# A scan layer's recurrence with part of its work on GpSimd, C turned ahead of it, and the last spectral pass with DRAM tiles of its own

## The chip, the cores and the metric

The kernel runs on one core of one Trainium2 chip. The metric is the device time of one execution in microseconds (us). TensorE (PE) multiplies matrices into PSUM, VectorE (DVE), ScalarE (ACT) and GpSimd (POOL) do the elementwise work, and SyncE (SP) issues most DMA transfers; ACT issues some.

## The reference

One image of 48 x 48 positions with 768 channels, f32, passes through four layers: an attention block, a spectral layer (a 2-D FFT, a two-layer network by blocks of 96 channels on every mode, the inverse FFT), a scan layer, and a second spectral layer with the same formula. What the change touches is the scan layer and the two spectral ones. The scan, shortened:

```python
B, C = silu(x @ W_B + ...), silu(x @ W_C + ...)      # 64 channels n x 4 ranks r
X = silu(x @ W_X + b_X);  alpha = sigmoid(x @ W_dec + b_dec)
theta = x @ W_th + b_th;  gamma = sigmoid(x @ W_lam + b_lam)
Hst, prev = 0, None
for i in range(12):
    inj = _rope(B, theta * (i + 1)) * X              # channel pairs turned by an angle
    Hst = diffuse(Hst)                               # 3x3 convolution, one filter per channel
    if prev is None: Hst = alpha * Hst + inj
    else: Hst = alpha * Hst + (1 - gamma) * alpha * prev + gamma * inj
    prev = inj
return silu((_rope(C, theta * 12) * Hst) @ W_out + b_out)
```

## The kernel before

The four layers follow one another on the core, and almost everything is f32. TensorE does the projections, the convolution (as products with banded matrices) and the FFTs (as products with matrices of sines). Instructions on each engine run in the order in which a scheduler puts them; `tc.keep_in_program_order` pins an instruction to its place in the program.

**Rows.** In the scan the 48 image rows lie in two halves on the partitions (48 columns at partition 0, 48 at partition 64, so 112 partitions are used, K), and 24 row pairs lie along the free axis (NPR).

**Projections** (`scan_phase`, line 1180 on). Eight chunks q of three row pairs each. TensorE writes a chunk's 357 columns for C, decay, angle, X and gamma and 256 for B into PSUM (line 1273); VectorE adds the biases into `za` and `g` (line 1274). Then the chunk's chain runs on VectorE and ScalarE: the angle is reduced and its sine and cosine are taken (`sincos`), g is multiplied by X (line 1299), B is turned by theta with `turn` (line 1475) into `i0` through two helper tiles m0 and m1, and H's first value is written (line 1310). Then the angle times 12 gets its own sine and cosine (from line 1311), and C with these is stored in DRAM as `c_d` (lines 1313, 1314). Last come the two states s0 and s1 (lines 1338 to 1344), with which the recurrence builds the injection without any more sines: the next state is `2 cos(theta) * s - previous s`.

**Recurrence** (`step` and `after`, lines 1364 to 1399). Eleven iterations `it` by eight groups `gr` of eight channels are 88 steps. A step is 64 recorded matmuls of H with the bands (line 1373), VectorE's product with alpha in PSUM (line 1375) and its sum with the state, written to H (line 1377). GpSimd forms `t = s * c1` (line 1381), ScalarE copies t over the PSUM bank just read (line 1382), and `after`, one step later, subtracts the older state (line 1393). There are four PSUM tiles, `pss[gr % 4]`. In the last iteration t and the subtraction fall away, and H is multiplied by the turned C (line 1399). The bands of groups 1 to 7 are loaded by SP just before the first step (line 1356), and ScalarE repeats alpha over the ranks into `alr`.

**C's turn by 12 theta** runs on GpSimd during the recurrence: `c_turned` loads a chunk from `c_d`, does `turn`'s six operations and stores `cr_d`; the loop over the steps advances it by one operation where `i % 4` is not zero. The last iteration reads `cr_d`.

**After the scan** comes the transposition of H (line 1443) and the output projection (line 1460).

**Spectral layers** (`spectrum_mix`). The FFT along the rows has put a spectrum into `yu` in DRAM. Items (group, kc, block) pass four stages with lags of 0, 1, 3 and 4 steps: FFT along the columns (line 1685), the two layers of the network (1699 to 1721), and the inverse (f_u, line 1736), evicted to `us` and handed to `put`. `keep_warm` (line 139) issues matmuls that nobody reads; three of them stand ahead of the first step, two at steps 1 and 2, and twelve behind the last step in `afno_second`. In `afno_second`, the last layer, each of four groups is two blocks of 96 channels; `put` stores a result to `yu` (line 1931), `reload` brings it back turned (line 1936) and `back` does the inverse FFT along the rows (line 1960) and stores the output (line 1950). For the final group the order of transfers is pinned; the second last kc's reload is issued together with the last one's:

```python
elif group == final and kc != NKC - 2:
    for k in (kc,) if kc < NKC - 1 else (kc - 1, kc):
        for b in range(2):
            reload(nc.scalar if k == NKC - 1 and b else nc.sync, b, chunk(k), 0, G // 2)
```

Of the kernel before, what the change touches and what calls it, by code (L numbers as in the profile page):

```python
# [21 lines left out]
G = 48  # L22
# [1157 lines left out]
def scan_phase(tc, ident, w, wts, rows_back, xh, x_close, c_d, cr_d, out_open):  # L1180
# [21 lines left out]
    NCR = NN * RR  # L1202
    NA = NCR + NN + NM + RR + 1
    V, GP = nc.vector, nc.gpsimd
    with tc.tile_pool(name="sc_s", bufs=1, side="left") as sp:
# [3 lines left out]
        def out_weights():  # L1209
            wp = out_open("so_w")  # L1210
            wo = wp.tile([P, 2, C], F32, tag="wo", name="wo")
            nc.sync.dma_start(wo, wo_d)
            return wo, load_bcast(nc, wp, bo_d, C, "bo", parts=K)

        with (
# [15 lines left out]
            with (  # L1231
                tc.tile_pool(name="sc_pw", bufs=1, side="left") as wp,
                tc.tile_pool(name="sc_pt", bufs=1, side="left") as tp,
            ):
                bias = load_bcast(nc, wp, b0_d, NA + NCR, "bias", pin=tc.keep_in_program_order)
                bias1 = load_bcast(nc, tp, b1_d, NA + NCR, "u", pin=tc.keep_in_program_order)
                V.tensor_tensor(bias, bias, bias1, ALU.add)
                cb = load_bcast(nc, wp, cb_d, NN, "cb", pin=tc.keep_in_program_order)
                halfpi = wp.tile([P, 1], F32, tag="halfpi", name="halfpi")
                V.memset(halfpi, math.pi / 2.0)  # L1240

                def temp(shape, tag, q, bufs=1):
                    return tp.tile([P, *shape], F32, tag=tag, name=f"{tag}_{q}", bufs=bufs)[:K]

                def sincos(th, q, nm):
                    r, a = reduce_angle(nc, tp, th, NM * R4, f"{nm}_{q}", K)
                    cs = temp([2, NM, R4], nm, q)
                    nc.scalar.activation(cs[:, 0].rearrange("p m t -> p (m t)"), a, AF.Sin, bias=halfpi[:K], scale=-1.0)
                    nc.scalar.activation(cs[:, 1].rearrange("p m t -> p (m t)"), r, AF.Sin)
                    return cs  # L1250

                def over_r(v, n):
                    return v.unsqueeze(2).to_broadcast([K, n, RR, R4])


                turn_of = itertools.cycle(range(2))
                banks = lambda tag: pss[3][:, next(turn_of), :]
                xs = [rows_back(0, banks)]
                for q in range(NQ):
                    prs = slice(q * R4, (q + 1) * R4)  # L1260
                    za = temp([NA, R4], "za", q, 2)
                    g = temp([NCR, R4], "g", q, 2)
                    for t in range(R4):
                        pr = q * R4 + t
                        if pr % 4 == 2 and pr + 4 < NPR:
                            xs.append(rows_back(pr // 4 + 1, banks))
                        x_of = lambda cc: (xs[pr // 4], cc, pr % 4 * P) if cc < NC // 2 else (xh, cc - NC // 2, pr * P)
                        ps = pss[pr % 3]
                        parts = ((za, 0, NA), (g, NA, NCR))
                        for i, (z, c0, n) in enumerate(parts):  # L1270
                            for cc in reversed(range(NC)):
                                v, c, tok = x_of(cc)
                                nc.tensor.matmul(ps[:K, i, :n], lhsT=v[:, c, tok : tok + K], rhs=w[:, cc, c0 : c0 + n], start=cc == NC - 1, stop=cc == 0)  # L1273
                        biased = [lambda z=z, c0=c0, n=n, i=i, t=t, ps=ps: V.tensor_tensor(z[:, :, t], ps[:K, i, :n], bias[:K, c0 : c0 + n], ALU.add) for i, (z, c0, n) in enumerate(parts)]
                        biased.pop(0)()
                        if t < R4 - 1:
                            biased.pop(0)()
                    last = q == NQ - 1
                    pin = tc.keep_in_program_order if last else lambda ins: ins

                    def silu():
                        pin(biased.pop(0)())
                        for t in (x, g, c):
                            pin(nc.scalar.activation(t, t, AF.Silu))

                    g3 = g.rearrange("p (n r) t -> p n r t", r=RR)
                    c, x = za[:, :NCR, :], za[:, NA - 1 - RR : NA - 1, :]
                    thz = za[:, NCR + NN : NCR + NN + NM, :]
                    alq = al[:K, :, prs]
                    ga = temp([1, R4], "ga", q)  # L1290
                    th = temp([NM * R4], "th", q)
                    if last:
                        silu()
                    V.tensor_copy(th, thz.rearrange("p m t -> p (m t)"))
                    cs = sincos(th, q, "t1")
                    if not last:
                        silu()

                    V.tensor_tensor(g.rearrange("p (n r) t -> p n (r t)", r=RR), g.rearrange("p (n r) t -> p n (r t)", r=RR), x.rearrange("p r t -> p (r t)").unsqueeze(1).to_broadcast([K, NN, RR * R4]), ALU.mult)
                    pin(nc.scalar.activation(alq, za[:, NCR : NCR + NN, :], AF.Sigmoid))  # L1300
                    pin(nc.scalar.activation(ga, za[:, NA - 1 : NA, :], AF.Sigmoid))
                    i0 = temp([NCR, R4], "i0", q)
                    i03 = i0.rearrange("p (n r) t -> p n r t", r=RR)
                    m = [temp([NM, RR, R4], f"m{j}", q) for j in range(2)]
                    for op in turn(V, i0, g, over_r(cs[:, 0], NM), over_r(cs[:, 1], NM), m):
                        op()

                    ac = temp([NN, R4], "ac", q)
                    V.tensor_tensor(ac, alq, cb[:K].unsqueeze(2).to_broadcast([K, NN, R4]), ALU.mult)
                    V.tensor_tensor(H[:K, :, :, 1 + q * R4 : 1 + (q + 1) * R4], i03, over_r(ac, NN), ALU.add)  # L1310
                    pin(V.tensor_scalar(th, th, float(ITERS), None, ALU.mult))  # L1311
                    cs12 = sincos(th, q, "t12")
                    nc.sync.dma_start(c_d[:K, q, :NCR], c)
                    nc.sync.dma_start(c_d[:K, q, NCR:].rearrange("p (s m) t -> p s m t", s=2), cs12)
                    c1q = c1[:K, :, prs]
                    pin(V.tensor_scalar(c1q, cs[:, 0], 2.0, None, ALU.mult))

                    def by_gamma(out, in_):
                        for t in range(R4):
                            nc.scalar.mul(out[:, :, t], in_[:, :, t], ga[:, 0, t : t + 1])  # L1320


                    om = temp([1, R4], "om", q)
                    pin(V.tensor_scalar(om, ga, -1.0, 1.0, ALU.mult, ALU.add))
                    be = temp([NN, R4], "be", q)
                    V.tensor_tensor(be, alq, om.to_broadcast([K, NN, R4]), ALU.mult)
                    bc = temp([NN, R4], "bc", q)
                    gc = temp([NM * R4], "th", f"{q}_g").rearrange("p (m t) -> p m t", t=R4)
                    V.tensor_tensor(gc, c1q, ga.to_broadcast([K, NM, R4]), ALU.mult)
                    for j in range(2):  # L1330
                        ms = slice(j * NM, (j + 1) * NM)
                        V.tensor_tensor(bc[:, ms], be[:, ms], gc, ALU.add)
                    flat = lambda v: v.rearrange("p n r t -> p (n r) t")

                    u = temp([NCR, R4], "u", q)
                    by_gamma(u, i0)
                    t0 = s0[:K, :, :, prs]
                    V.tensor_tensor(t0, g3, over_r(be, NN), ALU.mult)
                    V.tensor_tensor(flat(t0), flat(t0), u, ALU.add)
                    u = temp([NCR, R4], "u", f"{q}_1")  # L1340
                    by_gamma(u, g)
                    t1 = s1[:K, :, :, prs]
                    V.tensor_tensor(t1, i03, over_r(bc, NN), ALU.mult)
                    V.tensor_tensor(flat(t1), flat(t1), u, ALU.subtract)
            x_close()
            wo, bo = out_weights()
            with (
                tc.tile_pool(name="sc_h", bufs=1, side="right") as hp,
                tc.tile_pool(name="sc_t", bufs=6, side="right") as tp,
# [302 lines left out]
def spectrum_mix(tc, name, opened, psum, side, groups, put, beside):  # L1652
# [10 lines left out]
    with tc.tile_pool(name=f"{name}_s", bufs=2, side=side) as sp:  # L1663
# [86 lines left out]
        for step in range(len(items) + 4):  # L1750
            if 0 < step < 3:
                unread(2)
# [334 lines left out]
```

## Time and profile before

| | |
|---|---|
| median of 3 runs | 3557.33 us (3556.48 to 3559.4) |
| profiled execution, its own time | 3558.49 us |
| its span in the trace | 3556.6 us |
| mean granted TensorE clock | 0.995 |
| busy: PE, DVE, ACT, POOL | 3505.5, 2007.9, 1136.2, 683.4 us |
| scan: last projection matmul ends | 2972.64 |
| first step of the recurrence | 2980.99 |
| last step's matmuls end; first transpose of H | 3227.41; 3229.55 |
| first matmul of the last layer's spectral pass | 3321.51 |
| last put issued; inverse begins | 3531.29; 3542.91 |

Times in the trace count from the span's start. A row of a timeline is start, duration, engine, line, operation, output and inputs with their shapes; "x3" means that three neighbours are joined in one row, and the bracket tells how long the engine was idle before it and what ended that. A row of the chain of waits is start, duration and what the end waited for at that time. "PEclk" is the share of full TensorE speed that was granted. A busy PE is not always PE at its own pace, since matmuls are pipelined and their ends are modelled.

### The profile page before, as it was taken

The page shows a single profiled execution, that of the slowest core. Times are in us where ns is not written, and L with a number is a line of the kernel's source. Part 1 is how long each engine was busy: PE and PEld are TensorE (multiplying, and loading weights), DVE is VectorE, ACT ScalarE, POOL GpSimd, SP SyncE. Part 2 cuts the span into 40 slices and gives each one's busy share as a digit, 9 for nine tenths or more (in the row PEclk, how much of TensorE's full clock was granted, in tenths as well). Part 3 has the DMA queues.
Part 4 walks back from the last instruction along what each step waited for, and adds up shares of the span by engine and source line. Part 5 has one row for each costly group of instructions (what it writes and reads, how often), then busy time and mean ns, then how long its engine had stood idle before and what let it go on. Part 6 is the DMA issues. An engine that isn't in the chain of part 4 may idle for free.

```text
span 3556.6 us, 52951 instructions
## 1 busy us (share of the span) xinstructions
PE 3505.5 (99%) x21274; PEld 2145.6 (60%) x21274; DVE 2007.9 (56%) x3015; ACT 1136.2 (32%) x1733; POOL 683.4 (19%) x572
## 2 busy tenths in 40 slices
PE   9999999999999999999999999999999998999998
PEld 5666544444444444555555555555578777996686
DVE  7644466776776776574244314233245578995454
ACT  1222254555555555213101210120023265223332
POOL 3211102111111110340000000000023303981121
PEclk9999999999999999999999999999999999999999
DMA  8566546655545443443346334534544403104356
GB/s 286 196 207 199 191 143 184 174 160 140 161 122 150 123 126 87 152 149 114 106 140 184 105 108 143 151 111 126 145 127 112 110 20 106 35 27 104 103 144 133
DMA packets 281169, 480.36 MB, mean 135 GB/s; under 512 B 37250, under 2 KB 234466, under 8 KB 274708
## 3 DMA queue, kind: packets, MB, share of 16 engines
q1 hardware_dynamic: 265322, 455.95, 43.7%
q10 hardware_dynamic: 15594, 20.94, 2.0%
q8 instruction: 171, 2.80, 0.3%
q14 instruction: 82, 0.67, 0.1%
HBM read 330.82 MB, written 145.98 MB: 134 GB/s over the span
## 4 chain that ended last, share of the span: by engine, by line
PE 90%; DVE 3%; DMA 3%; ACT 2%; POOL 1%; issue 1%; SPq 0%; ACTq 0%; DVEq 0%; POOLq 0%
PE p L1111 14%; PE p L1048 14%; PE s L685 12%; PE av L716 11%; PE qk L391 6%; PE c L1273 4%; PE pj L186 3%; PE c L1373 3%; PE s L695 3%; PE v L186 3%; PE f_u L1736 2%; PE so L1460 2%; PE f_z L1721 2%; PE f_z L1720 2%; PE f_x L1685 2%; PE f_o L1699 1%
## 5 line engine op out<-in xcount | busy, mean ns | idle before, releaser
L705 DVE TENSOR_TENSOR acc<-acc,p 128x928 f32<-128x928 f32 (+1 forms) x480 | 561.0, 1169 | 259.4 <-ACT p L697 218.2
L697 ACT ACTIVATE p<-s 128x928 f32<-128x928 f32 (+1 forms) x540 | 505.4, 939 | 489.4 <-PE s L695 467.5
L685 PE MATMUL s<-qt,kv 64*128 64x464 f32 (+1 forms) x2160 | 516.7, 555 | 5.2 <-DMA k_d<-kT 2.9
L1111 PE MATMUL p<-w,h 128*128 128x384 f32 x1512 | 492.3, 487 | 0.0
L716 PE MATMUL av<-p,kv 128*64 128x464 f32 (+1 forms) x2160 | 442.6, 554 | 0.0
L1111 PEld LDWEIGHTS p<-w,h 128*128 128x128 f32 x1512 | 286.0, 190 | 198.6 <-issue 4.2
L695 PE MATMUL s<-bt,oneh 64*128 64x464 f32 (+1 forms) x1080 | 396.1, 728 | 0.0
L716 PEld LDWEIGHTS av<-p,kv 128*64 128x64 f32 x2160 | 147.0, 137 | 261.2 <-issue 249.8
L685 PEld LDWEIGHTS s<-qt,kv 64*128 64x128 f32 x2160 | 199.3, 186 | 164.4 <-issue 152.0
L1048 PE MATMUL p<-x2nT,w 128*128 128x384 f32 x864 | 291.0, 487 | 0.9 <-DVE pj_o L195 0.9
L1373 PE MATMUL c<-H,bands 128*48 128x96 f32 x5632 | 244.6, 247 | 10.2 <-DVE th L1311 8.3
L391 PE MATMUL qk<-xnT,wqk 128*128 128x384 f32 x756 | 253.4, 488 | 0.6 <-DMA wqk<-wqk_d 0.6
L1373 PEld LDWEIGHTS c<-H,bands 128*48 128x48 f32 x5632 | 234.8, 123 | 20.1 <-issue 8.7
L1048 PEld LDWEIGHTS p<-x2nT,w 128*128 128x128 f32 x864 | 164.0, 190 | 116.9 <-DVE h L1070 2.4
L1048 PE MATMUL p<-xT,w 128*128 128x384 f32 x648 | 220.8, 486 | 0.0
L1087 POOL TENSOR_TENSOR rr<-rr,ml_b 128x1152 f32<-128x1152 f32 x12 | 33.4, 2784 | 928.7 <-DMA rr<-xr_d 651.6
L1043 ACT ACTIVATE h<-h,ml_b 128x384 f32<-128x384 f32 x144 | 88.4, 614 | 351.4 <-DVE h L1063 178.0
L391 PEld LDWEIGHTS qk<-xnT,wqk 128*128 128x128 f32 x756 | 139.9, 190 | 88.5 <-issue 1.8
L1381 POOL TENSOR_TENSOR t<-s,c 128x768 f32<-128x768 f32 x80 | 144.3, 1826 | 180.8 <-DMA bands<-in_bands_dram 168.3
L1048 PEld LDWEIGHTS p<-xT,w 128*128 128x128 f32 x648 | 123.3, 190 | 85.7
L695 PEld LDWEIGHTS s<-bt,oneh 64*128 64x128 f32 x1080 | 103.9, 187 | 104.8 <-issue 104.6
L1721 PE MATMUL f_z<-f_w,f_o 97*96 97x96 f32 x800 | 133.4, 248 | 0.0
(336 smaller groups left out, 4616.6 us busy)
## 6 DMA issues: line engine op xcount, KB each, us to landing
w<-w1s_d SPq DMA_DIRECT2D x36, 768.0 KB
w<-w2s_d SPq DMA_DIRECT2D x36, 768.0 KB
w<-w1s_d SPq DMA_DIRECT2D x36, 576.0 KB
w<-in_mlp_w_dram SPq DMA_DIRECT2D x27, 768.0 KB
yu<-f_ys SPq DMA_DIRECT2D x48, 384.0 KB
wqk<-wqk_d SPq DMA_DIRECT2D x12, 1344.0 KB
bt<-rw_d SPq DMA_DIRECT2D x72, 174.0 KB
bt<-rh_d SPq DMA_DIRECT2D x72, 174.0 KB
```

Source lines behind the costliest of these rows:

```text
L186: nc.tensor.matmul(p[:, :TB], lhsT=rhs[n][:, c, t * P : (t + 1) * P], rhs=w[:, c, :], start=c == 0, stop=c == NC2 - 1)
L391: nc.tensor.matmul(p[:, :TB], lhsT=w[:, n, c, :], rhs=ops[sb][n][:, c, :], start=c == 0, stop=c == NC2 - 1)
L685: nc.tensor.matmul(ps[:, s, :n], lhsT=keys[pr % 2][rows, kt * P : (kt + 1) * P], rhs=held(c)[rows, :n], start=True, stop=False)
L695: nc.tensor.matmul(ps[:, s, :n], lhsT=oneh[rows, b % 2, :], rhs=bts[b // 2][rows, j, :n], start=False, stop=True)
L697: nc.scalar.activation(p, ps[:, :, :n], AF.Exp)
L705: nc.vector.tensor_tensor(probs[c], probs[c], p, ALU.add)
L716: nc.tensor.matmul(avs[c][rows, : size(c)], lhsT=vals[pr % 2][:, kt, rows], rhs=p[:, s, :], start=kt == 0, stop=kt == NT - 1)
L1048: nc.tensor.matmul(p[:, :TB], lhsT=w[n][:, c, :], rhs=rhs[n][:, c, :], start=c == 0, stop=c == NC2 - 1)
L1111: nc.tensor.matmul(ps[t][:, :TB], lhsT=hs[left, f][:, t * P : (t + 1) * P], rhs=wt[:, f % KW2, :], start=f == 0, stop=f == NF2 - 1)
L1373: nc.tensor.matmul(ps[r0 : r0 + G, k // 4, cols], lhsT=bands[:, n - GC, i, :] if gr else bands0[:, n, i, :], rhs=H[:, n, :, d : d + NPR], ...
L1381: GP.tensor_tensor(t, sc[:, ch], c1[:, m0 : m0 + GC].unsqueeze(2).to_broadcast([P, GC, RR, NPR]), ALU.mult)
L1721: nc.tensor.matmul(out, lhsT=o1[:, j, 0:2, :].rearrange("c r h -> c (r h)"), rhs=w2t[:, b, 1, :], start=False, stop=True)
```

## The change

1. **Recurrence.** In groups 3 and 7 (`APART`) GpSimd itself subtracts the older state, and ScalarE's copy falls away there; VectorE's three operations are pinned in the order of the program (product, H, subtraction of the step before).
2. **C.** For chunks 0 to 5 C is turned in place by GpSimd in the projections (`turn_in_place`), through the same single pair of tiles m0 and m1 that VectorE's turn uses, and goes to `cr_d` directly. Only the last two chunks (`LATE`) pass through `c_d` and are turned in the recurrence, one operation where `i % 4 == 1`.
3. **Last chunk.** The second state is formed first; the first one after step 0; sine and cosine of 12 theta at step 2. The bands are loaded before C's store, and the weights of the output projection at step 8. Fourteen unread matmuls stand before the first step.
4. **Spectral passes.** The three unread matmuls ahead fall away in both layers, and for the last layer two are put ahead of each of the last two steps.
5. **Ways back of the last layer.** Each group has its own DRAM tile, so that the reload's row is contiguous (18,432 bytes for the final group instead of pieces of 768), and each kc of the final group is reloaded right after its put.

The core of the diff (regrouped pools and lines that only move in are left out):

```diff
+    LATE = 2
...
-                    cs12 = sincos(th, q, "t12")
-                    nc.sync.dma_start(c_d[:K, q, :NCR], c)
-                    nc.sync.dma_start(c_d[:K, q, NCR:]..., cs12)
+                def end_turn():
+                    pin(V.tensor_scalar(th, th, float(ITERS), None, ALU.mult))
+                    cs12 = sincos(th, q, "t12")
+                    if q >= NQ - LATE:
+                        if not last:
+                            nc.sync.dma_start(c_d[:K, q - NQ + LATE, :NCR], c)
+                        nc.sync.dma_start(c_d[:K, q - NQ + LATE, NCR:]..., cs12)
+                    else:
+                        mc = [temp([NM, RR, R4], f"m{j}", f"c_{q}") for j in range(2)]
+                        for op in turn_in_place(GP, c, over_r(cs12[:, 0], NM), over_r(cs12[:, 1], NM), mc):
+                            op()
+                        nc.sync.dma_start(cr_d[:K, q], c)
+                if not last:
+                    end_turn()
...
+                if not last:
+                    first_state()
...
+            keep_warm(tc, pss[3][:, 0], flat_bands[:, :96], flat_bands[:, :384], 14)
...
+                nc.sync.dma_start(c_d[:K, LATE - 1, :NCR], c)      # behind the bands' loads
+                APART = (3, 7)
...
-                        nc.scalar.copy(pv, t...)
+                        if gr in APART:
+                            sn = s[(it + 1) % 2][:, ch]
+                            GP.tensor_tensor(sn, t, sn, ALU.subtract)
+                        else:
+                            nc.scalar.copy(pv, t...)
...
-                turns = (op for q in range(NQ) for op in c_turned(q))
+                turns = (op for q in range(NQ - LATE, NQ) for op in c_turned(q))
                 for i in range(len(steps) + 1):
                     if i < len(steps):
                         step(*steps[i])
-                    if i % 4:
+                    if i == 0:
+                        first_state()
+                    if i % 4 == 1:
                         next(turns, int)()
                     if i:
                         after(*steps[i - 1])
+                    if i == 2:
+                        end_turn()
+                    if i == NG:
+                        load_out()
...
+def turn_in_place(eng, v, co, si, m):
+    v = v.rearrange("p (j m r) t -> p j m r t", j=2, r=RR)
+    a, b = v[:, 0], v[:, 1]
+    for args in ((m[0], b, si, ALU.mult), (m[1], a, si, ALU.mult), (a, a, co, ALU.mult), (a, a, m[0], ALU.subtract), (b, b, co, ALU.mult), (b, b, m[1], ALU.add)):
+        yield lambda args=args: eng.tensor_tensor(*args)
...
-        unread(3)
         for step in range(len(items) + 4):
-            if 0 < step < 3:
+            if 0 < step < 3 or alone and step > len(items) + 1:
                 unread(2)
...
+        backs_d = [dp.tile([KR, G, W], F32, tag=f"yb{n}", name=f"yb{n}") for n in range(len(groups))]
...
-            pin(nc.sync.dma_start(spectrum_of(yu[half], kc, cs), us))
+            pin(nc.sync.dma_start(spectrum_of(backs_d[group], kc, slice(0, W)), us))
...
-            elif group == final and kc != NKC - 2:
-                for k in (kc,) if kc < NKC - 1 else (kc - 1, kc):
+            elif group == final:
+                for b in range(2):
+                    reload(nc.scalar if kc == NKC - 1 and b else nc.sync, b, chunk(kc), 0, G // 2)
```

## The prediction

> **What bounds the kernel now.** I read the page first, then the waits of TensorE, then the timelines of the places that the diff touches.
>
> ```profile
> PE 3505.5 (99%) x21274; PEld 2145.6 (60%) x21274; DVE 2007.9 (56%) x3015; ACT 1136.2 (32%) x1733; POOL 683.4 (19%) x572
> PE 90%; DVE 3%; DMA 3%; ACT 2%; POOL 1%; issue 1%; SPq 0%; ACTq 0%; DVEq 0%; POOLq 0%
> ```
>
> TensorE is busy almost always, so most of the 3557 us can't move: a gain must come from a hole in PE, from PE at half clock, or from a stretch in which PE counts as busy while something else sets its pace. Its waits, where the diff reaches (us in total, times, longest):
>
> ```profile
> PE c L1373 <- DVE th L1311: 8.3, 1, 8.3
> PE f_w L1960 <- DMA f_gt<-yu: 4.6, 1, 4.6
> ...
> PE f_first L139 <- issue: 1.8, 1, 1.8
> ```
>
> The third kind is the recurrence. Its steady state, in the timelines of VectorE and of ScalarE (start, duration):
>
> ```profile
> 3058.52 0.95 DVE L1377 TENSOR_TENSOR H<-c,s 128x768 f32<-128x768 f32 x1
> 3059.38 0.95 DVE L1375 TENSOR_TENSOR c<-c,alr 128x768 f32<-128x768 f32 x1
> 3060.41 0.96 DVE L1393 TENSOR_TENSOR s<-c,s 128x768 f32<-128x768 f32 x1
> 3061.28 0.95 DVE L1377 TENSOR_TENSOR H<-c,s 128x768 f32<-128x768 f32 x1
> ```
> ```profile
> 3059.57 0.80 ACT L1382 COPY c<-t 128x768 f32<-128x768 f32 x1 [1.96 <-DVE H L1377]
> ```
>
> A step recurs every 2.76 to 2.77 us (3058.52 to 3061.28). The loop is: H ends at 3059.47, the copy of t into PSUM runs 3059.57 to 3060.37, the subtraction follows at 3060.41, and the next H 0.87 behind it. VectorE has no gap and ScalarE's copy sits between H and the subtraction. In the last iteration there is no copy and no subtraction, and the pace changes:
>
> ```profile
> 3224.81 0.97 DVE L1375 TENSOR_TENSOR c<-c,alr 128x768 f32<-128x768 f32 x1 [0.68 <-PE c L1373]
> ...
> 3227.45 0.97 DVE L1375 TENSOR_TENSOR c<-c,alr 128x768 f32<-128x768 f32 x1 [0.68 <-PE c L1373]
> ```
>
> Here VectorE waits for PE, and a step takes 2.64. So PE could go at 2.64, and the loop of DVE and ACT holds it at 2.77.
>
> The way into the recurrence, in windows (PE, PEld, DVE, ACT, POOL busy, granted clock, DMA share, GB/s):
>
> ```profile
> 2975.00:2985.00 10.00, 4.01 (x51) 4.04 (x53) 9.11 (x26) 9.03 (x18) 0.00 (x0) 0.50 0.94 365
> 2985.00:2990.00 5.00, 5.00 (x124) 5.00 (x122) 3.75 (x5) 4.84 (x9) 0.39 (x1) 0.98 0.77 261
> ```
>
> The projections' last matmul ends at 2972.64, H is ready at 2980.85, and the steps start at 2980.99 at clock 0.50, which lasts until 2985.3: 4.3 us at half speed lose 2.15.
>
> **Part 1, the recurrence section**, from 2972.64 to the first transpose of H at 3229.55: 256.9 us before.
> The chain of VectorE that ends in the last chunk's H is not touched, so H comes at about 2980.9 as before. The 14 matmuls that nobody reads start at once; such a matmul takes 0.658 (7.90 for 12 in the tail), so they last 9.2, end at 2981.85, and hold PE 0.9 beyond H. For this the clock stays at 1.00.
> Per step afterwards VectorE has product, H and the subtraction of the step before, in this fixed order: ACT's copy has a product and an H to hide behind, so no gap is left. A dense step is 2.73 (0.99 from product to H, 0.87 twice); in groups 3 and 7 without a subtraction it is 1.86 (0.99 + 0.87). Mean (6 x 2.73 + 2 x 1.86) / 8 = 2.51, below PE's 2.64. PE becomes the pace if GpSimd keeps up. Its durations, by form:
>
> ```profile
> L1381 POOL TENSOR_TENSOR t<-s,c x80: 1807/1824/1853, 2989.6 to 3196.4; 128x768 f32<-128x768 f32 x80
> L1475 POOL TENSOR_TENSOR cr<-cr,m x16: 988/1007/1035, 3000.4 to 3174.4; 112x384 f32<-112x384 f32 x16
> ```
>
> The apart subtraction, 128x768 on GpSimd, isn't in the trace. Lower bound 1.82 (the product of the same shape), upper bound 3.8 (twice the 1.89 of the slow rows below). I take 2.0, twice the 1.007 of a two-input operation on half the elements beside the very same VectorE work. Then GpSimd has 8 x 1.83 + 2 x 2.0 = 18.6 per eight steps against 8 x 2.64 = 21.1; the 12 turning operations left (11.5 in all, instead of 48) fit in the rest. It would become the pace only from 3.2 on (21.1 - 14.6, halved).
> Added waits: the bands go ahead of the store of C, so GpSimd's first product and ACT's first copy wait for that store, which stands behind seven loads of 786 KB in SP's queue; at the 412 to 442 GB/s at which these flow before, 5.5 MB take some 13 us, and the product starts at 2988.5 to 2990 (2989.61 before). Behind it on GpSimd are the later products, and PE's fifth and later steps wait for the subtractions they feed; first_state's two operations behind step 0 wait for ACT's eight copies of alr. I take 1.7 us of stalls in the first ten steps; 0 if everything hides, 5 if the store lands two steps late. The weights of the output projection move to step 8 and are needed 220 us later; the six queue entries are free.
> Sum: 9.2 + 88 x 2.645 + 1.7 + 2.14 (last H to transpose, as before) = 245.8. **-11.1 us** (bounds -13 to -8 by the stalls).
>
> **Part 2, C turned in the projections.** 36 operations of GpSimd that has nothing else there (not one in the window 2945 to 2975). Six of 0.93 to 1.01 are 5.8 us per chunk. They start when the second sine is there, 12.2 us after the chunk's arrival, and share m0 and m1 with VectorE's own turn, which the next chunk wants 23.6 to 26.6 us after it: 11.4 us or more for 5.8. What covers this is the idle time of VectorE, 3.8 us per chunk waiting for PE. Price 0; if that cover is gone, six chunks at up to 5.8 - 3.8 = 2.0 of delay plus 1.7 of half clock each, +22. What speaks against it is the only place where GpSimd and VectorE collide now:
>
> ```profile
> 546.23 1.00 POOL L151 TENSOR_TENSOR pw0p<-pw0b,pw0p 128x384 f32<-128x384 f32 x1 [109.98 <-DMA bt<-rh_d]
> 547.18 1.89 POOL L153 TENSOR_TENSOR pw0p<-pw0p,pw0b 128x384 f32<-128x384 f32 x1
> ...
> 547.09 4.81 DVE L705 TENSOR_TENSOR acc<-acc,p 128x928 f32<-128x928 f32 x3 [2.04 <-ACT p L697]
> ```
>
> One operation goes from 1.00 to 1.89 as soon as VectorE adds two operands from SBUF, and VectorE's own addition takes up to 1741 ns there against 1125 where GpSimd is idle. Even at 1.89 the six take 11.3, just inside 11.4. In the recurrence each VectorE operation has one operand in PSUM, and the product on GpSimd stays at 1.82 beside it, so I carry no such price there.
> The Trainium skill has this in "GPSIMD Engine Reference", section "8. Key points": GpSimd shares its SBUF interfaces with VectorE and contends with VectorE instructions that have two SBUF inputs. The row 1.00 to 1.89 agrees; by that rule the projections (gate product, both states) would pay and the recurrence would not.
>
> **Part 3, the spectral passes.** The three unread matmuls ahead go. At L3's start they stand in the way:
>
> ```profile
> 3321.51 2.58 PE L139 MATMUL f_first<-f_w,f_fh 96*96 96x384 f32 x6 [1.79 <-issue]
> 3323.88 1.81 PE L1685 MATMUL f_x<-f_fh,f_yt 96*96 96x96 f32 x10
> ```
>
> Three of them cover 3321.51 to 3323.88 = 2.37; without them f_x starts that much earlier: **-2.3**, bounds -3.5 (the clock stays up too) and 0 (f_yt is late, or a longer hole halves the clock for one window more). At L1's start PE waits 2.7 us for f_yt after them anyway: 0, at worst +1.7 by half clock.
> The clock rule in "TensorE: Matmul & The Clock Gate", section "Part 1: The HAM clock gate", has a free-running window of 3413 ns and a drop only after an idle window. In this trace a hole of 1.8 us at 3319.7 was followed by 0.50 from 3323.3 to 3326.5; by the page the removal of cover would cost nothing, by the trace up to 1.7, which the bounds hold.
>
> **Part 4, the tail.** The chain of waits at the end:
>
> ```profile
> 3531.29 3.32 DMA yu<-f_us
> ...
> 3534.63 8.04 DMA f_gt<-yu
> ...
> 3542.91 6.94 PE f_w L1960 x48
> ```
>
> After the last put four reloads of 184 KB run, in pieces of 768 B, for 8.04. Afterwards kc 3's pair goes ahead of the last put, and the two left read whole rows of 18,432 B. If bytes alone set it, half of 8.04 is 4.0, landing at 3538.7; if they go at the rate of the put (360 KB in 3.32), 3.3, at 3537.9. The 12 unread matmuls hold PE until 3538.35 in any case. So f_w starts at 3538.4 to 3539 instead of 3542.91; and no hole of 4.6 us means that it doesn't fall to the clock of 0.50 (48 at full clock: 3 x 1.52 = 4.56 instead of 6.94). But the twelve stores behind are bound by their own transfer, some 8.7 us from the first (3546.4) to the last (3555.0), so what counts is when the first third of f_w ends: 3545.42 before, about 3540.3 after. **-5.2** (bounds -5.5 and 0). The two pairs of unread matmuls added near the end lie in the 1.5 and 1.4 us that PE waits there for Z (a pair is 1.31): 0. Own tiles as such remove no wait; the order and the shape of the reloads do.
>
> **Sum.** -11.1 - 2.3 - 5.2 = -18.6. The profiled execution took 3558.49 (span 3556.6 and 1.9 around it), 1.16 over the median of 3557.33: 3539.9 on its basis, 3538.7 on the median's. About 0.2%, 7 us, is what a measurement of this kernel can tell from no change.
>
> **Rivals.**
> *Contention in the recurrence, slower than before.* GpSimd's apart subtraction takes 3.8, and VectorE's operations beside it stretch by the ratio of part 2 (1741 against 1125 ns, 0.55). Then VectorE has 20.1 + 2 x 3.8 x 0.55 = 24.3 per eight steps, 3.04 per step; 88 x (3.04 - 2.645) = +35, net +16: 3573. It decides from 1.0 us of stretch per eight steps on. For: 547.18. Against: the product with two SBUF inputs at 1.82 beside VectorE at 0.95 all along. Chance 0.07.
> *The subtraction slow on GpSimd alone.* 14.6 + 7.6 = 22.2 per eight steps, 2.78 per step: +11.9, the whole gain of the steps, 3550. Chance 0.09.
> *The projections overrun.* +22 as above, 3561. Chance 0.05.
> *The tail keeps its length* if two reloads of ten long rows take as long as four of 240 short pieces did: 3544. For: the trace has no reload of such rows; before, the time need not have gone with the bytes. Chance 0.10.
> The case of the sum has the remaining 0.69.
>
> **How the numbers follow.** Predicted 3539. Low end: stalls 0, -3.5 and -5.5 in the other parts, and steps of 2.60: 3539 - 1.7 - 1.2 - 0.3 - 4 = 3531.8, say 3531. High end 3550, which takes in the lost tail and about half of the slow subtraction. Outside are 0.07 + 0.05 + 0.04. Faster: 0.69 + 0.10 + half of 0.09, 0.84; within 0.2%: the other half and the overrun, 0.09; slower 0.07.
>
> **What would show it.** Right: steps 2.64 apart with VectorE waiting for PE, the apart subtraction near 2.0, clock 1.00 at the first step, f_w behind the unread matmuls at full clock, first store near 3527 (3540.3 less the 13.4 gained ahead of it). Wrong: GpSimd without idle time in the steps, VectorE's operations longer than 0.97, waits of PE for za's bias additions in the projections, or f_gt still last before f_w.

## The result, and the profile after

The changed kernel is slower: median 3565.38 us (3559.93 to 3570.92, 14 runs) against 3557.47 (3552.81 to 3560.27, 14 runs), ratio 1.0021, interval 1.0013 to 1.0029. Its profiled execution took 3564.43, with a span of 3562.5. All executions of one kernel spread over some 10 us, so stretches below are compared within the traces, by what PE did at their ends:

| stretch, us | before | after | change | forecast |
|---|---|---|---|---|
| start to the projections' last matmul | 2972.64 | 2975.13 | +2.5 | 0 |
| to the first step | 8.35 | 9.64 | +1.3 | +0.85 |
| first step to the steps' end | 246.42 | 249.02 | +2.6 | -11.9 |
| to the last matmul of the output's rows (so_f) | 92.31 | 92.26 | -0.1 | 0 |
| to the second item of the last layer (f_o) | 11.97 | 10.07 | -1.9 | -2.3 |
| to the last f_u | 198.89 | 198.89 | 0 | 0 |
| to the end of the span | 26.02 | 27.49 | +1.5 | -5.2 |
| sum | 3556.6 | 3562.5 | +5.9 | -18.6 |

Of the 24.5 us between forecast and traces, 14.5 lie in the steps, 6.7 in the tail and 2.5 ahead of the projections' end.

The page's first line, and PE's longest waits (us in total, times, longest):

```profile
PE 3504.9 (98%) x21298; PEld 2145.9 (60%) x21298; DVE 2012.8 (56%) x2995; ACT 1120.7 (31%) x1713; POOL 735.0 (21%) x592
```
```profile
PE c L1401 <- DVE H L1405: 13.2, 1, 13.2
PE f_x L1731 <- DMA f_yt<-yu: 6.0, 1, 6.0
PE f_w L2003 <- DMA f_gt<-yb: 5.1, 2, 4.5
...
PE c L1869 <- DVE x L71: 2.9, 2, 1.8
```

The wait of 8.3 ahead of the first step is gone, as forecast, and one of 13.2 has taken its place after the third. The three variants below that leave the order of the steps as it is show this hole too, of 11.7 to 16.7 us. What VectorE and GpSimd did in it, from their timelines:

```profile
2999.43 0.94 DVE L1320 TENSOR_SCALAR th<-th 112x96 f32<-112x96 f32 x1
3000.41 1.73 DVE L1168 TENSOR_SCALAR t_k<-th 112x96 f32<-112x96 f32 x1
3002.18 1.76 DVE L1169 TENSOR_SCALAR t_k<-t_k 112x96 f32<-112x96 f32 x1
3003.97 3.56 DVE L1170 SCALAR_TENSOR_TENSOR t_r<-t_k,th 112x96 f32<-112x96 f32 x1
3007.56 1.74 DVE L1171 SCALAR_TENSOR_TENSOR t_r<-t_k,t_r 112x96 f32<-112x96 f32 x1
3009.33 1.74 DVE L1172 SCALAR_TENSOR_TENSOR t_r<-t_k,t_r 112x96 f32<-112x96 f32 x1
3011.10 2.64 DVE L1174 TENSOR_SCALAR t_r<-t_r 112x96 f32<-112x96 f32 x1
```
```profile
3002.02 1.84 POOL L1412 TENSOR_TENSOR s<-t,s 128x768 f32<-128x768 f32 x1
3003.78 0.96 POOL L1521 TENSOR_TENSOR m<-c,sc 112x384 f32<-112x384 f32 x1
3004.67 1.83 POOL L1409 TENSOR_TENSOR t<-s,c 128x768 f32<-128x768 f32 x1
3006.43 0.95 POOL L1521 TENSOR_TENSOR cr<-c,sc 112x384 f32<-112x384 f32 x1
3007.31 3.65 POOL L1409 TENSOR_TENSOR t<-s,c 128x768 f32<-128x768 f32 x2
3010.92 1.00 POOL L1521 TENSOR_TENSOR cr<-cr,m 112x384 f32<-112x384 f32 x1
```

These are the seven small operations that reduce the last chunk's angle times 12, put behind step 2 by the change. Before, when GpSimd was idle, each took 0.20 to 0.26 us; some of them:

```profile
2980.76 0.20 DVE L1311 TENSOR_SCALAR th<-th 112x96 f32<-112x96 f32 x1
...
2981.49 0.26 DVE L1170 SCALAR_TENSOR_TENSOR t_r<-t_k,th 112x96 f32<-112x96 f32 x1
```

Here four of them last about as long as a product of GpSimd (1.83), one twice as long, and they end 0.1 to 0.2 us behind a change of GpSimd from one operation to the next, as far as the joined rows show it (3002.0, 3003.8, 3007.3, 3010.9). Together they take 14.3 us instead of 1.6, with every product and H of the steps queued behind them on VectorE.

The way into the steps, in windows (columns as before):

```profile
2975.00:2985.00 10.00, 9.40 (x35) 4.64 (x35) 8.37 (x23) 7.97 (x15) 0.00 (x0) 1.00 0.89 343
...
3000.00:3015.00 15.00, 2.42 (x60) 2.22 (x54) 14.76 (x9) 1.20 (x2) 15.00 (x12) 0.66 0.01 2
3015.00:3020.00 5.00, 4.33 (x71) 4.33 (x73) 4.93 (x6) 1.72 (x4) 4.92 (x4) 0.64 0.57 147
```

The clock is at 1.00 where it was 0.50, and the hole has moved to 3000, with GpSimd busy all through it. The half clock has moved along: the trace has 0.50 from 3004.9 to 3018.6, so that the first 3 us behind the hole run at half speed too.

The steady state, further on, is what was forecast:

```profile
3049.03 0.97 DVE L1403 TENSOR_TENSOR c<-c,alr 128x768 f32<-128x768 f32 x1 [0.34 <-PE c L1401]
...
3059.59 0.97 DVE L1403 TENSOR_TENSOR c<-c,alr 128x768 f32<-128x768 f32 x1 [0.34 <-PE c L1401]
```
```profile
L1412 POOL TENSOR_TENSOR s<-t,s x20: 1792/1856/1865, 3002.0 to 3199.4; 128x768 f32<-128x768 f32 x20
```

Four steps in 10.56, 2.64 each, VectorE waiting for PE, and the subtraction on GpSimd at 1.86. Beside that GpSimd, VectorE's operations with one operand in PSUM stay at 0.97.

### The profile page after: what moved, and what is told of

Its sections match the earlier page's. It is cut to its first block, busy times and chain, and to the rows that moved or that the text cites. A ratio compares the mean times of both kernels' runs of the same rounds, so it can differ in the third digit from the quotient of the medians.

```text
span 3562.5 us, 52960 instructions
## 1 busy us (share of the span) xinstructions
PE 3504.9 (98%) x21298; PEld 2145.9 (60%) x21298; DVE 2012.8 (56%) x2995; ACT 1120.7 (31%) x1713; POOL 735.0 (21%) x592
## 5 line engine op out<-in xcount | busy, mean ns | idle before, releaser
L1401 PE MATMUL c<-H,bands 128*48 128x96 f32 x5632 | 234.7, 246 | 14.9 <-DVE H L1405 13.2
```

Source lines behind the costliest of these rows:

```text
L1401: nc.tensor.matmul(ps[r0 : r0 + G, k // 4, cols], lhsT=bands[:, n - GC, i, :] if gr else bands0[:, n, i, :], rhs=H[:, n, :, d : d + NPR], ...
```

## The experiments

All ratios are to the kernel before, run on the same chip; the changed kernel's is 1.0021.

**The seven operations behind step 0 instead of step 2.**

```diff
                     if i == 0:
                         first_state()
+                        end_turn()
...
-                    if i == 2:
-                        end_turn()
```


> Edit: of the changed kernel, the last chunk's sine and cosine of 12 theta (seven short operations of VectorE with all operands in SBUF) are formed after step 0 instead of after step 2, that is before GpSimd's first product; nothing else moves. Theory A (such an operation gets through only between two operations of GpSimd, so that each of the seven lasts as long as a GpSimd product, 1.7 to 3.6 us instead of 0.2): the seven take 0.2 to 0.26 each, PE's hole of 13.2 us after the third step is gone, some 1.5 us of it come back as a later product of step 1; 11 to 14 us faster than the changed kernel, about 3552. Rival B (the hole comes from the store of C behind the bands' loads, and from the products that wait for it): the hole stays within 2 us of its length and the time within 0.1%. Rival C (GpSimd is too slow for the steps once it subtracts): the hole is spread over the following steps instead, and the time stays.

Measured: ratio 0.9999 (0.999 to 1.0008), some 8 us faster than the changed kernel, and the longest wait 9.7 instead of 13.2. The steps take 244.5 instead of 249.0. Neither theory's number, but the trace decides. VectorE's timeline, then GpSimd's:

```profile
2992.69 0.21 DVE L1320 TENSOR_SCALAR th<-th 112x96 f32<-112x96 f32 x1
2992.93 0.21 DVE L1168 TENSOR_SCALAR t_k<-th 112x96 f32<-112x96 f32 x1
2993.17 1.87 DVE L1169 TENSOR_SCALAR t_k<-t_k 112x96 f32<-112x96 f32 x1
2995.08 1.78 DVE L1170 SCALAR_TENSOR_TENSOR t_r<-t_k,th 112x96 f32<-112x96 f32 x1
```
```profile
2993.16 8.90 POOL L1409 TENSOR_TENSOR t<-s,c 128x768 f32<-128x768 f32 x5 [36.62 <-DVE t_k L1168]
```

Two operations pass at 0.21; at 2993.16 GpSimd starts its five products, and the third, 0.01 later, takes 1.87. I had taken GpSimd to be idle for long enough; it was so for 0.5 us.

**Added operations in the middle of the recurrence**, in the kernel of the first experiment.

```diff
+                    if i in (24, 32, 40, 48, 56):   # four of one kind at each
+                        pin(V.tensor_scalar(d[:, :96], gf[:, :96], 2.0, None, ALU.mult))
+                        ...
```


> Edit: the kernel of the first run, with four added operations of VectorE that write scratch at each of five steps in the middle of the recurrence, where GpSimd is never idle: multiplication by a constant 112x96, product of two SBUF operands 112x96, scalar_tensor_tensor of two SBUF operands 112x96, multiplication by a constant 112x768, product of two SBUF operands 112x768. Alone these last 0.2 to 0.26, and about 0.5 to 1.0. Theory A (VectorE has to wait for the end of GpSimd's operation whenever all its operands are in SBUF): all five kinds last 1 to 2 us each. Rival B (only the operations with a constant, which move one operand, are held off): the products stay under twice their time alone. Rival C (nothing of this: the seven operations were slow through something else of that place): all at their time alone.

Measured, by line (minimum, median and maximum in ns):

```profile
L1463 DVE TENSOR_SCALAR i<-g x4: 1432/1793/3483, 3063.1 to 3068.2; 112x96 f32<-112x96 f32 x4
L1465 DVE TENSOR_TENSOR i<-g x4: 248/1762/1827, 3092.0 to 3096.0; 112x96 f32<-112x96 f32 x4
L1467 DVE SCALAR_TENSOR_TENSOR i<-g x4: 257/258/289, 3117.9 to 3118.8; 112x96 f32<-112x96 f32 x4
L1469 DVE TENSOR_SCALAR i<-g x4: 560/1338/2093, 3139.2 to 3142.6; 112x768 f32<-112x768 f32 x4
L1471 DVE TENSOR_TENSOR i<-g x4: 948/1712/2492, 3166.0 to 3170.5; 112x768 f32<-112x768 f32 x4
```

Theory A, in one execution: one input or two, 96 columns or 768. The third kind fell by chance into a gap of GpSimd (3118.06 to 3118.96), and took 0.26, so this run doesn't test it; it is the kind of lines 1170 to 1172, which took 1.74 to 3.56 in the changed kernel. The wait goes both ways: a GpSimd product that began while VectorE's 768 columns ran took 2.55 instead of 1.83. The four of the first kind lasted 8.61 together, and the steps behind them came that much later.

**All seven ahead of the first step.**

```diff
+            cs12_last = end_turn()          # behind the last chunk's second state
             flat_bands = ...
...
                     if i == 0:
                         first_state()
+                        nc.sync.dma_start(c_d[:K, LATE - 1, NCR:]..., cs12_last)
...
-                    if i == 2:
-                        end_turn()
```


> Edit: of the changed kernel, the last chunk's sine and cosine of 12 theta are formed ahead of step 0, right behind the second state, where GpSimd has nothing; only the store of the pair stays behind step 0. Theory A (an operation of VectorE with all operands in SBUF waits for GpSimd's operation to end; the run with the seven operations behind step 0 still met GpSimd's products, which began 0.5 us after the first of the seven): all seven last 0.2 to 0.26, PE has no wait over 4 us in the first ten steps, the section from the first to the last step takes 236 to 240 instead of 249.0; 9 to 13 us faster than the changed kernel, some 0.1 to 0.2% faster than before. Rival B (the store of C behind the bands holds up the steps whatever VectorE does): a hole of 8 us or more is still there.

Measured: median 3548.2, ratio 0.9979 (0.9969 to 0.9989): 15 us faster than the changed kernel and faster than before. The seven take 0.20 to 0.26; only the last operation of the first state, behind step 0, still meets GpSimd's first product and takes 2.47. PE's waits from 2975 to 3225:

```profile
PE ht L1484 <- DVE H L1408: 2.2, 1, 2.2
PE c L1404 <- issue: 1.9, 1, 1.9
PE c L1404 <- DVE s L1429: 1.3, 1, 1.3
```

First step to steps' end: 236.3; the forecast for the changed kernel was 232.8 + 1.7. Theory A, and rival B falls: the store of C is where it was. With it the hole of the changed kernel is explained by the placing of seven short operations alone.

**GpSimd subtracts nothing**, in that kernel.

```diff
-                APART = (3, 7)
+                APART = ()
```


> Edit: as the run with the sine ahead of step 0, and all eight groups take ScalarE's copy and VectorE's subtraction; GpSimd subtracts nothing. Theory A (the prediction's price of the steps): VectorE is dense at 2.73 per step and PE waits for it; the section from the first to the last step is 70 to 80 x 0.09 = 6 to 7 us longer than with groups 3 and 7 on GpSimd. Rival B (what paces the steps before is VectorE's order alone, and PE can't go under 2.73): no difference over 2 us.

Measured: 1.0001 (0.9993 to 1.001), the steps 242.7 instead of 236.3. The quarter on GpSimd is worth 6.4 us, as priced. Rival B falls.

**No turn of C in the projections.** This kernel leaves the turn of six chunks out, so its output lacks it.

```diff
-                        for op in turn_in_place(GP, c, ...):
-                            op()
```


> Edit: of the changed kernel, GpSimd's turn of C in the projections is left out for chunks 0 to 5 (C is stored as it is, so the output lacks that turn); the recurrence is untouched. Theory A (GpSimd beside VectorE's additions of two SBUF operands lengthens these, PSUM is emptied late, and PE waits some 3.5 us for it): PE's waits for evictions of the rows that come back fall from 3.9 us to under 1, and the time by 2 to 3.5 us. Rival B (the 2.4 us lost up to the projections' end come from the unread matmuls missing at the first spectral layer): no change beyond 0.03%. Rival C (projections overrun as priced in the prediction): 20 us faster.

Measured: 1.0006 (0.9997 to 1.0015), some 5 us faster than the changed kernel. From the first f_x to the projections' end 378.8; before it was 379.0. With the six chunks turned there, ten traces (the changed kernel and its variants) show 380.7, 380.9, 381.0, 383.3, 383.5, 384.1, 384.4, 384.7, 384.8 and 385.0. The three shortest are the three without a half clock of 3.4 us near 2803, which the trace of before and those without the turn have (from 2804.5 to 2807.5 the granted clock was 0.50 before and 1.00 in the changed kernel); so the fair comparison is that of the other seven, 383.3 to 385.0, with 378.8 to 379.4. What VectorE's subtraction for the second state takes (mean in ns), first without, then with the turn on GpSimd beside it (groups of the two kernels):

```profile
L1364 DVE TENSOR_TENSOR s<-s,u 112x768 f32<-112x768 f32 x7 | 7.2, 1034 | 2.1 <-ACT u L1336 1.9
```
```profile
L1367 DVE TENSOR_TENSOR s<-s,u 112x768 f32<-112x768 f32 x7 | 10.8, 1543 | 2.1 <-ACT u L1339 2.0
```

What GpSimd's own operations take there, 112x384, in the changed kernel (minimum, median, maximum in ns):

```profile
L1509 POOL TENSOR_TENSOR m_c<-za,t x12: 927/1784/2727, 2839.9 to 2951.0; 112x384 f32<-112x384 f32 x12
```

Theory A, at about twice its price: PE waits 3.8 us for the evictions of the rows that come back, against 0.5, and a hole of 1.8 to 2.5 us near 2885 was followed by a half clock of 3.4 us in four of the traces (not in the changed kernel's own, which has the hole too).

**All of C turned in the recurrence, one group on GpSimd**, from the kernel with the seven ahead of the first step.

```diff
-    LATE = 2
+    LATE = 8
-                APART = (3, 7)
+                APART = (7,)
-                    if i % 4 == 1:
+                    if i % 4:
```


> Edit: as the run with the sine ahead of step 0, and C of all eight chunks is turned in the recurrence as before the change (48 operations, where i % 4 is not zero); to make room for them on GpSimd only group 7 is subtracted there. VectorE then has (7 x 2.73 + 1.86) / 8 = 2.62 per step, GpSimd 80 x 1.83 + 10 x 1.85 + 48 x 0.95 = 210.5 of 211: both just at PE's pace. Theory A (C's turn in the projections costs 2 to 5 us through VectorE's lengthened additions, and the steps lose less than that): 2 to 4 us faster than the run with the sine ahead of step 0. Rival B (GpSimd at its limit becomes the pace of the steps): 3 us or more slower than that run.

Measured: 1.0008 (0.9999 to 1.0017), some 10 us slower than the kernel it came from: rival B. The stretch up to the projections' end is 379.4, as without the turn, but the steps take 250.6. GpSimd's rate is not all of it: its products waited 9.6 us for `cr_d<-cr` to land, because the turned chunks take their tiles from the same six as t. PE waited 10.9 for subtractions.

**Four chunks in the recurrence**, from the kernel with the seven ahead of the first step.

```diff
-    LATE = 2
+    LATE = 4
-                    if i % 4 == 1:
+                    if i % 8 in (1, 4, 6):
```


> Edit: as the run with the sine ahead of step 0, with C of the last four chunks instead of two turned in the recurrence (24 operations, where i % 8 is 1, 4 or 6); groups 3 and 7 stay on GpSimd. GpSimd then has 80 x 1.83 + 20 x 1.85 + 24 x 0.95 = 206 of 211. Theory A (each chunk turned in the projections costs VectorE and so PE 0.4 to 1 us there): the stretch from the first f_x to the projections' end shrinks by 1 to 2 us and the steps lose under 1.5; 0 to 2 us faster than the run with the sine ahead of step 0. Rival B (GpSimd near its limit holds up the steps, as in the run with all eight chunks there): the steps lose 3 us or more and the sum is slower by 1 to 4 us.

Measured: 0.998 (0.9971 to 0.999); 380.9 from the first f_x to the projections' end (without the half clock near 2803), steps 237.3. No difference from two chunks that these runs can tell.

**The old way back**, in the changed kernel.

```diff
-            pin(nc.sync.dma_start(spectrum_of(backs_d[group], kc, slice(0, W)), us))
+            pin(nc.sync.dma_start(spectrum_of(yu[half], kc, cs), us))
...
-            elif group == final:
+            elif group == final and kc != NKC - 2:
```


> Edit: of the changed kernel, the last layer's way back is as before: one shared DRAM tile with pieces of 768 bytes, and the second last kc's reload issued together with the last one's. Theory A (in SP's order the reload ahead of the last put makes it wait for the landing of the put before, 1 us, and its long rows then share the transfer with that put): 1.5 to 2 us faster than the changed kernel, from the last f_u to the inverse 12.3 instead of 14.1. Rival B (the stretch varies from run to run, and the new order is worth the 5 us that were forecast in most runs): 3 to 5 us slower.

Measured: 1.0019 (1.001 to 1.0028), the same as the changed kernel: rival B's 3 to 5 us don't show, and theory A's 1.5 to 2 are too few for these runs. From the last f_u to the span's end 26.0, as before.

**Own tiles, old order.**

```diff
-            elif group == final:
-                for b in range(2):
+            elif group == final and kc != NKC - 2:
+                for k in (kc,) if kc < NKC - 1 else (kc - 1, kc):
```


> Edit: of the changed kernel, the final group's second last kc is reloaded together with the last one as before, but from its own DRAM tile in rows of 18,432 bytes. Theory A (SP's reload ahead of the last put delays that put): the last put starts within 0.1 us after its operand is ready and lands 3.3 after; the four reloads of long rows then take 6 to 8 us; from the last f_u to the inverse 11 to 12.5. Rival B (long rows are what slows the reload, a row of 18,432 bytes taking 1.7 to 2.2 us by itself): four reloads take over 8 us, and the stretch is longer than before's 12.3.

Measured, in one execution: the last put lands 3.56 after its start, as in the old order, and the chain ends

```profile
3537.83 3.56 DMA yb<-f_us
...
3541.46 8.33 DMA f_gt<-yb
```

so four reloads in rows of 18,432 bytes take 8.33; in pieces of 768 they took 8.04 before. Theory A is right on the put, rival B on the reloads: here the shape of the rows brings nothing. The changed kernel's own chain:

```profile
3528.94 6.97 DMA yb<-f_us
3535.92 0.27 SPq L1980
...
3536.66 5.98 DMA yb<-f_us
...
3542.71 6.23 DMA f_gt<-yb
```

The operand of the last put was ready at 3535.70; SP, waiting for the put before it to land, issued it at 3536.66; beside the reloads it took 5.98; and two reloads still took 6.23. The inverse began 12.2 after the last f_u, against 12.3 before, and the half clock behind that hole is there again (0.50 from 3547.6, before from 3541.5).

That trace is one of a wide spread. In the ten traces with the new order of puts and reloads (without the next experiment's), the last put took 4.0 to 6.6, against 3.0 to 3.6 in the three with the old order; the two reloads behind it took 4.3 to 6.6, against 8.0 to 8.4 for four. Put and reloads together come to 10.0 to 12.5, against 11.4 to 11.9, and from the last f_u to the span's end it is 23.5 to 27.5, against 25.8 to 26.0. None comes near the 20.8 that were forecast.

**The second last reload on ScalarE's queue**, from the kernel with the seven ahead of the first step.

```diff
-                    reload(nc.scalar if kc == NKC - 1 and b else nc.sync, b, ...)
+                    reload(nc.scalar if kc == NKC - 2 or kc == NKC - 1 and b else nc.sync, b, ...)
```


> Edit: as the run with the sine ahead of step 0, with the second last kc's reload in the final group issued by ScalarE's queue instead of SP's. Theory A (SP stands waiting for the landing of the put before, with the last put behind it): the last put starts within 0.1 us of its operand in every run; it still shares the transfer with the reload, 4 to 6 us; from the last f_u to the inverse 10 to 11.5 us, 0 to 1.5 us faster than the run with the sine ahead of step 0. Rival B (the put is slow by the long rows beside it alone): nothing gained.

Measured: 0.9978 (0.9969 to 0.9987), no difference from the kernel it came from (0.9979). The put was issued at once (3521.90, operand at 3521.87) but took 6.15, and the last reload 6.51: rival B. What SP's wait costs this run can't tell, since in the trace of the kernel it came from SP issued the put at once as well (3521.70, operand at 3521.67; the put took 5.16).

**No unread matmuls ahead of the steps**, from the same kernel.

```diff
-            keep_warm(tc, pss[3][:, 0], flat_bands[:, :96], flat_bands[:, :384], 14)
```


> Edit: as the run with the sine ahead of step 0, without the fourteen unread matmuls ahead of the first step. Theory A (they keep the clock up, as priced in the prediction): granted clock 0.50 for some 4 to 10 us after 2975 and again 1.00 behind, first step 0.6 to 1 us earlier, the section from the first to the last step 2 to 5 us longer; 1 to 4 us slower. Rival B (the first steps wait for other things anyway, so that the half clock costs nothing): no difference beyond 0.03%.

Measured: 0.9976 (0.9967 to 0.9985). The clock does fall, to 0.50 from 2981.0 for 10.2 us, and the steps take 236.0 all the same: rival B. With the unread matmuls the ratio was 0.9979.

**The silu table loaded ahead**, from the same kernel.

```diff
                 if last:
+                    pin(nc.scalar.activation(ahead, halfpi, AF.Silu))
                     silu()
...
-            keep_warm(..., 14)
+            keep_warm(..., 12)
```


> Edit: as the run with the sine ahead of step 0, with a silu of one constant column on ScalarE ahead of the last chunk's silus, so that the table is loaded before the chunk arrives, and with twelve unread matmuls instead of fourteen, so that they end before H. Theory A (H of the last chunk came 1.3 us later than before because the load of the silu table, 1.28, stood behind the wait for the chunk's biases): from the projections' end to the first step 8.2 to 8.5 instead of 9.6, the steps as long as in the run with the sine ahead of step 0; 1 to 1.5 us faster than that run, about 0.9975 of before. Rival B (the first steps wait for GpSimd's first product, which follows the store of C behind the bands at a fixed time): the first step is earlier, but the section from the first to the last step is longer by the same amount.

Measured: 0.9977 (0.9968 to 0.9986), no difference in time. The first step comes 8.70 after the projections instead of 9.61, so the table's load (1.28 in the trace) was most of the 1.3; the steps are no longer for it (236.5), but 0.9 us is below what these runs can tell. In the three traces where GpSimd turns no C shortly ahead of it (the two without any turn in the projections and the one with four chunks in the recurrence), ScalarE loads that table ahead of its wait without that change, and the step comes after 8.96, when the fourteen unread matmuls are done.

## Why the prediction was wrong, point by point

- **The step that failed** is part 1's "Added waits". I counted what the moved pieces wait for and who waits for the store of C, but the seven operations of the last chunk's angle, moved from a place where GpSimd was idle to one where it is not, have no price in the sum. "I take 1.7 us of stalls in the first ten steps": the steps took 249.0, 16.2 more than the 232.8 of their pace, 13.2 of it in one hole. GpSimd's first product, which waits for the store of C, came at 2993.1 and not at 2988.5 to 2990; that delay is still there in the kernel with the seven ahead, whose steps take 3.5 more than the pace. Beside it I wrote that in the recurrence "each VectorE operation has one operand in PSUM"; that holds for the steps and not for these seven. The rows 1.00 to 1.89 that I showed were read as a ratio, a slowing to half for as long as both run. The experiments show a wait for the other's whole operation, so that the shortest lose most: 0.21 to 1.8.
- **The Trainium skill** had the rule I needed: "SBUF — State Buffer", section "Who interferes with whom", says that a VectorE operation in a two-port mode (a multiplication by a constant can enter one), or with two SBUF inputs, contends with GpSimd for a shared pair of ports, and that this pair is an exclusive lock: in a two-port mode whoever issues first has it for the whole instruction, and the other is blocked. The rows at 2993.16 and 2993.17 agree, 1.87 against a product of 1.83; in which mode VectorE ran, no run shows. I had cited the shorter notice in "GPSIMD Engine Reference", which names the two-port modes as well; I kept only its half on two SBUF inputs, and applied that to the steps only.
- **Part 2**, C's turn in the projections, was priced at 0 with a bound of 22. By the traces that are alike near 2803 it costs some 4 to 6 us (383.3 to 385.0 against 378.8 to 379.4). My cover, 3.8 us of idle time per chunk on VectorE, is a sum over the chunk; the row copies stand where there is none. The contention was named there, with the wrong size.
- **Part 4**, the tail, -5.2 forecast, +1.5 measured, -2.5 to +1.5 over the ten traces. The fourth rival, the tail keeping its length, was the case, though not by its condition alone. The sum took 3.3 to 4.0 for two reloads and the put as it was: the reloads took 6.2 (4.3 to 6.6 over the traces), and the put beside them 6.0 instead of 3.3. So half the bytes took less time, but mostly not half, and what was put ahead was paid for by the put beside it. What makes these transfers vary from run to run stays open.
- **The warm matmuls** held the clock and gained nothing: the first steps wait for VectorE and for GpSimd's first product (2993.1) anyway. In the kernel with the seven ahead, the 2.15 us that I gave for the half clock are no part of the path.
- "The chain of VectorE that ends in the last chunk's H is not touched" was 1.3 us off, 0.9 of it through the silu table's place on ScalarE.
- **Right** were the pace of the steps (2.64, VectorE at 2.73 and 1.86, the subtraction 1.86 for a forecast 2.0), its worth (6.4 us measured by undoing it), and part 3 (-1.9 for -2.3: the first f_x follows the last so_f after 1.8 us instead of 4.2). With the seven operations put where GpSimd is idle, the step part alone gives 246.4 - 236.3 = 10.1 of the forecast 11.9. The whole kernel then gains 0.2%, some 7 us, and not 18.6: the projections' loss takes a part, and the tail's gain isn't there.

The slower rival that I priced, contention in the recurrence, named the right two engines and the wrong operations; the steps' own are untouched by it.

## What to carry to other kernels

Before moving a short operation into a loop where GpSimd is always busy, look at where its operands lie: with all of them in SBUF each one waited for a whole operation of GpSimd here, so seven of 0.2 us cost 14. Give such work a place where GpSimd is idle; the steps' own operations, with one operand in PSUM, weren't held up. Of a transfer on the path, ask whether its time goes with its bytes at all, before shortening it or putting another beside it.

## What was not expected of the hardware

The wait of VectorE and GpSimd for each other goes by whole operations and in both directions (VectorE 0.21 to 1.87, GpSimd 1.83 to 2.55). The last two reloads of 184 KB, in ten rows each, took 4.3 to 6.6 us from issue to landing, although a row's packet shows 1.1 to 2.3 us in the changed kernel's trace. And the half clock of 10 us under the first steps cost nothing that the runs can tell (0.9976 with it, 0.9979 without), since PE was not what these steps waited for.
